# Issuing the transfers of SyncE's queue in written order, and placing loads, stores and the pieces of W1, W3 and W2 elsewhere in a step

## The chip, the cores and the metric

The kernel runs on one core of one Trainium2 chip. The metric is the device time of one execution in microseconds (us). The engines are TensorE (PE in the profile; its weight loads are PEld), VectorE (DVE), ScalarE (ACT), GpSimd (POOL) and SyncE (SP), which only issues transfers (DMAs).

## The reference

The model is one post-norm layer: gated slot attention, a layernorm over the residual sum, a gated FFN with a Hadamard transform, and a second layernorm. The input x has 2 batches of 2048 rows of 512 values, all fp32. The attention has 16 heads with 64 key features, 64 slots and 128 value features.

```python
q, k = heads(x @ Wq), heads(x @ Wk)                  # 64 wide
v = heads(x @ Wv); s = clip(heads(x @ Ws), -32, 32)  # 128 values, 64 slots
z = cumlogsumexp(s, time); g = exp(z_prev - z); p = exp(s - z)
hk = hk * g + k p^T;  ok = (q / 8) @ hk              # per time step
pv = softmax(ok)
hv = hv * g + p v^T;  o = pv @ hv                    # per time step
gate = x @ Wg
o = o * rsqrt(mean(o^2) + eps) * g_norm * silu(gate)
x = layernorm(x + o @ Wo)
h = fwht(silu(x @ W1^T) * (x @ W3^T))                # hidden 2048
out = layernorm(x + h @ W2^T)
```

## The kernel before

**Products of large matrices.** The projections, the output projection and the FFN's products are done in fp32 by a scheme with seven half-size products instead of eight. Each factor is cut in four blocks; VectorE forms sums of blocks of the weights and of x ahead of time (`first_sums`, `second_sums`, `right_sums`, `Weights.sums` at L408 and the lines beside it), TensorE makes the seven products in the order 1, 5, 6, 2, 7, 3, 4, and `Unit.into` takes each result from its PSUM bank: products 1, 5, 6 and 4 by ScalarE's copy, products 2, 7 and 3 by one VectorE addition each (L464) of the kept block. There are few PSUM banks for these, so a late addition holds a later product.

**Steps.** The 16 heads are done in NG = 4 groups of four, and the 2048 rows of time in NCB = 16 chunks of 128, for both batches at once. A group and a chunk make one `Step`, 64 in all, in order of groups. `run(new, now, before, old)` interleaves four steps. For `now` it makes the projections of q, k and the slot scores (`q(k)`, products at L504) and of v and the gate (`v(k)`, L530). For `new` it loads x and in the first group makes its block sums (`load_x`, `make_x`) and stores them to DRAM (`xd`, L488), from where later groups load them ready. For `before` it makes the gate, the softmax and the values. For `old` it makes the output projection (`o(k)`, L801), which adds to the partial rows: in the first group these are x itself, later the rows stored by the group before in `yd` (`load_rows` L748, `store_rows` L817).

**The burst.** Between product 1 and product 5 of v lies a run of small matmuls on 64x64 tiles: `scores` (L591), `scores2` (L681), `share_of_keys` (L607), `share_of_values` (L697), `slots` (L627), `values` (L710), `state_slots` (L636) and `state_values` (L719). These are 512 instructions of TensorE, matmuls and weight loads together, and take some 5 us. Keys, exponentials and weights need transposed copies for it. They are made by DMA transposes on 16-bit halves: GpSimd writes the halves (`parts`), SyncE issues the transpose (`rt` at L673, `kt` at L553, `et` at L564, `ot` at L769), ScalarE joins the halves (`kr` at L557). L607 is the first user of `kr`. `running_sum` also stores the last row of the running sum for the next step (`zc`, L579).

**Pieces.** Work that belongs to the FFN's weights is cut into pieces: generators that do some instructions and yield. `work()` runs them in order and `work_on(place)` takes the next one, at place 1 (in the q products), 2 (between q2 and q7), 3 (in the v products) and 4 (after v4). `up_weights` loads W1 and W3 in pieces of 1 MB (`both`), forms the block sums on VectorE (`outer`, `inner`) and stores them to DRAM (`w13s`, L853 to L856); it lies in the first group and the beginning of the second. `down_weights` multiplies W2 with a 128x128 Hadamard matrix (`product`, L909, 16 matmuls), does the other four butterfly levels on VectorE (L933, L935), forms the block sums (L941 to L944) and stores them (`w2s`); it lies in the second and third group. `block(j)` prepares the FFN's input from the normalised rows in the last group, with block sums on VectorE named `halves`. The FFN follows behind the last step (`up` at L238, `down` at L277).

**What sets the order.** The attention part stands in a block `tc.manual_schedule(engines={PE, DVE, Activation, Pool})`: on these four engines instructions are issued in the order in which the program writes them. SyncE is not in the set, so a scheduler of the build decides the order of the transfers on SyncE's queue by its own costs. An engine's queue is in order: an instruction that waits holds all behind it. The tail of the FFN has a second block of the same kind, which stays as it is.

The weights of the next group (`load_qks`, `load_vg`, `load_o`; `Weights` at L401, of which `low` is a shared buffer of one slot) are loaded when the group's last step comes (`last`; `o_last` for the output projection, two steps later), and the first step of a later group is called `changes`.

Of the kernel before, what the change touches and what calls it, by code (L numbers as in the profile page):

```python
# [24 lines left out]
NG = H // HG  # L25
# [14 lines left out]
def gated_slot_attention_ffn_kernel(  # L40
# [13 lines left out]
    nc = tc.nc  # L54
# [298 lines left out]
    with ExitStack() as att:  # L353
# [112 lines left out]
        class Step:  # L466
# [17 lines left out]
            def make_x(self):  # L484
                if self.g:
                    return
                right_sums(self.xb, self.b12)
                nc.sync.dma_start(out=xd[self.n], in_=self.xb)  # L488


            def q(self, k):
# [346 lines left out]
        def up_weights():  # L838

            todo = [(p, i) for p in range(NSET) for i in range(2)]  # L840

            def load(n):

                p, i = todo[n]
                nc.scalar.dma_start(out=both[:, n % 2].rearrange("p h q a b t -> p (h q a b t)"), in_=w13t[i, p])

            def inner(d, src, at, n):

                t = hp.tile([P, 4, 2, P], F32, name="inner", tag="h3", bufs=4)[:, :, 0:n]
                first_sums(nc.vector, t, *(src(r, c) for r in range(2) for c in range(2)))  # L850
                o = d[:, at : at + n].rearrange("p m k t -> p k m t")
                for c in range(2):
                    nc.sync.dma_start(out=o[:, c], in_=src(0, c))  # L853
                nc.sync.dma_start(out=o[:, 2], in_=src(1, 1))
                for k in range(4):
                    nc.sync.dma_start(out=o[:, 3 + k], in_=t[:, k])  # L856

            def sums(d, wt):

                outer = hp.tile([P, 4, 2, 2, P], F32, name="outer", tag="h2")  # L860
                a11, a12, a21, a22 = (wt[:, r, :, c] for r in range(2) for c in range(2))
                nc.vector.tensor_tensor(outer[:, 0], a21, a22, ALU.add)
                nc.vector.tensor_tensor(outer[:, 2], a11, a21, ALU.subtract)
                yield
                nc.vector.tensor_tensor(outer[:, 1], outer[:, 0], a11, ALU.subtract)
                nc.vector.tensor_tensor(outer[:, 3], a12, outer[:, 1], ALU.subtract)
                yield
                inner(d, lambda r, c: wt[:, 1, r, 1:2, c], 2, 1)
                yield
                inner(d, lambda r, c: outer[:, 0:2, r, c], 3, 2)  # L870
                yield
                inner(d, lambda r, c: outer[:, 2:4, r, c], 5, 2)
                yield
                inner(d, lambda r, c: wt[:, 0, r, :, c], 0, 2)

            both = hp.tile([P, 2, 2, 2, 2, 2, P], F32, name="both", tag="h1")
            rest = iter(())
            load(0)
            for n, (p, i) in enumerate(todo):
                for half in range(2):  # L880
                    for place in range(4):

                        if place == 3 and half:
                            for _ in rest:
                                pass
                            rest = sums(w13s[p][:, :, :, i], both[:, n % 2])
                        if place != 2:
                            next(rest, None)
                        if place == 3 and half and n + 1 < len(todo):
                            y["load"] = lambda n=n: load(n + 1)  # L890
                        yield
            for place in range(4):
                if place != 2:
                    next(rest, None)
                yield
            for place in range(4):
                if place != 2:
                    next(rest, None)
                yield

        def down_weights():
# [3 lines left out]
            for pair in ((0, 2), (1, 3)):  # L905
                wh = hp.tile([P, 2, NFB, P], F32, name="wh", tag="h1")

                def product(n, raw):
                    nc.tensor.matmul(bank(0), lhsT=hm, rhs=raw.rearrange("p (c t) -> p c t", t=P), start=True, stop=True)  # L909
                    nc.scalar.copy(wh[:, n // 4, n % 4 * 4 : n % 4 * 4 + 4], bank(0))  # L910
# [8 lines left out]
                for n in range(8):  # L919
                    yield  # L920
                    yield
                    yield
                    nraw = load(n + 1) if n < 7 else None
                    yield
                    product(n, raw)
                    raw = nraw
                for i in range(2):
# [127 lines left out]
        def run(new, now, before, old):  # L1055
# [13 lines left out]

            def work_on(place):  # L1070

                if changes or (last and place > 2) or (o_last and place == 3):
                    return
                y["place"] = place
                next(pieces[0], None)
# [25 lines left out]
            if new is not steps[1]:  # L1101
                do(new, "load_x")
            do(before, "tanh")
            main("q", 5)
            do(before, "squared_sums")
            do(before, "silu")
            y["second"] = new is not None and new.g > 0
            work_on(1)
            main("q", 6)
            if crossed:  # L1110
                old.o_joined()
# [6 lines left out]
            if crossed:  # L1118
                old.o_sums(True)
            main("q", 4)  # L1120
            if last:
                nw["qks"] = load_qks(g + 1)
            if now is steps[-1]:
                wt.append(load_w(0, 0))
                open_x("wqks", OUTER[:3], 3 * P)
# [25 lines left out]
                old.o(3)  # L1151
            do(old, "row_stats", 1)
            do(old, "o", 4)
            if old is not None and old.g < NG - 1:
                old.store_rows()
            do(now, "k_joined")
            y.pop("load", lambda: None)()
            if o_last:
                nw["o"] = load_o(old.g + 1)
            do(before, "load_rows")  # L1160

            do(now, "reciprocal", 0)
            do(now, "open_shares")
# [20 lines left out]
            do(before, "scaled")  # L1184

            do(old, "row_stats", 0)
            main("v", 5)
            for f in late:
                f(2)
# [12 lines left out]
            do(now, "softmax")  # L1202
            if old is not None and old.g == NG - 1:
                old.normalize()
                old.store_rows()
            if before is not steps[-1]:
                do(before, "o_split")
            do(now, "r_scaled")
            do(now, "r_split")
            if last:  # L1210
# [3 lines left out]
                for k in range(4):  # L1214
                    nw["o"].sums(k)
            main("v", 3)
            work_on(3)
            more()
            if before is steps[-1]:
                before.o_transposed()  # L1220
# [23 lines left out]
                    pieces[0] = chain(pieces[0], block(old.n // 4))  # L1244

        with tc.manual_schedule(
            engines={mybir.EngineType.PE, mybir.EngineType.DVE, mybir.EngineType.Activation, mybir.EngineType.Pool}
        ):
            steps[0].load_x()
            nw["qks"] = load_qks(0)  # L1250
            steps[1].load_x()
            nw["vg"] = load_vg(0)
            nw["o"] = load_o(0)
            steps[0].make_x()
            for k in range(4):
                nw["qks"].sums(k)
            N = len(steps)
            for i in range(N + 2):
                if i == N:
                    open_x("wvg", OUTER[3:], 4 * P)  # L1260
                    open_acc("ux", tag="h1")
                    ups = up(0, h)
                run(*(steps[j] if 0 <= j < N else None for j in (i + 1, i, i - 1, i - 2)))
            for _ in pieces[0]:
                pass
# [110 lines left out]
```

## Time and profile before

| | us |
|---|---|
| median of 3 runs | 3507.64 |
| lowest and highest run | 3504.44, 3511.28 |
| the profiled execution | 3514.42 |
| its span, first to last instruction | 3512.6 |
| mean granted TensorE clock in it | 0.988 |
| first matmul, end of the second step | 8.7, 85 |
| end of the first, second, third, last group | 642, 1212, 1791, 2383 |

How to read the profile: times count from the span's start. In a window's row the columns are start:end and length, then busy us and instructions of PE, PEld, DVE, ACT and POOL, the granted TensorE clock, the busy share of the core's 16 DMA engines, and GB/s. A row of waits names an engine, what it was about to write and the line, what it waited for, then us in total, times, longest. "issue" means that the engine waited for nothing that the profile shows. A row of the timeline has start, duration, engine, line, operation, out<-in, and in brackets the idle time ahead of it and what ended it. SPq is SyncE's queue: its durations are those of issuing, not of the transfer.

### The profile page before, as it was taken

To read this page: it belongs to the slowest core of one execution; us is meant where nothing else is said; L and a number is where in the kernel's file an instruction comes from. 1 tells how busy PE (TensorE), PEld (TensorE's weight loads), DVE (VectorE), ACT (ScalarE), POOL (GpSimd) and SP (SyncE) were. 2 spreads that over 40 slices of the span, in tenths; PEclk is the share of its full clock that TensorE was granted. 3 is DMA by queue.
4 is the path that set the end of the run, shared out by engine and by line. 5 is a ranking of instruction groups with operands and counts; after the bars stand their busy time and mean duration, and the time that the engine had idled before them with its cause. 6 is when DMAs were issued, how large, how long until landed. Compare 5 with 4: busy or idle time off the path is not lost.

```text
span 3512.6 us, 74754 instructions
## 1 busy us (share of the span) xinstructions
PE 3334.4 (95%) x30440; PEld 2631.8 (75%) x30440; DVE 2292.2 (65%) x3769; ACT 1306.4 (37%) x2939; POOL 1579.5 (45%) x1429
## 2 busy tenths in 40 slices
PE   7988988999999999999999999988999999999998
PEld 5766666777677766777677776766888888888887
DVE  4666656776556765556777677777666756756756
ACT  3444444454554554555455544542111111111110
POOL 2443444444444444444454444443634643643544
PEclk9999999999999999999999999999999999999999
DMA  5555555644443544434354565577455544445431
GB/s 170 145 154 145 144 143 151 175 120 119 93 108 92 149 111 116 104 97 106 95 150 112 123 161 158 163 204 254 172 180 206 176 160 177 154 154 182 163 135 68
DMA packets 542632, 508.40 MB, mean 145 GB/s; under 512 B 353488, under 2 KB 454224, under 8 KB 541264
## 3 DMA queue, kind: packets, MB, share of 16 engines
q1 hardware_dynamic: 541136, 495.23, 48.4%
q10 hardware_dynamic: 1152, 8.39, 0.8%
q8 instruction: 240, 3.93, 0.5%
q14 instruction: 104, 0.85, 0.1%
HBM read 297.47 MB, written 125.30 MB: 120 GB/s over the span
## 4 chain that ended last, share of the span: by engine, by line
PE 79%; DVE 9%; ACT 4%; issue 4%; DMA 2%; POOL 1%; SPq 0%; DVEq 0%; POOLq 0%; ACTq 0%
PE c L238 18%; PE c L530 18%; PE dc L277 11%; PE c L801 10%; PE c L504 9%; ACT r L654 2%; PE sp L719 2%; PE sp L710 2%; DVE t L464 2%; PE pv L697 2%; PE ps L573 1%; DMA kt<-parts 1%; PE ps L636 1%; PE sp L591 1%; DVE t L544 1%
## 5 line engine op out<-in xcount | busy, mean ns | idle before, releaser
L530 PE MATMUL c<-wvg,xb 128*128 128x512 f32 x1792 | 806.1, 601 | 7.8 <-DVE t L464 3.4
L530 PEld LDWEIGHTS c<-wvg,xb 128*128 128x128 f32 x1792 | 338.4, 192 | 396.8 <-issue 382.4
L504 PE MATMUL c<-xb,wqks 128*128 128x128 f32 x3584 | 556.5, 278 | 58.3 <-DVE t L464 45.4
L504 PEld LDWEIGHTS c<-xb,wqks 128*128 128x128 f32 x3584 | 477.2, 192 | 97.4 <-issue 55.1
L219 DVE TENSOR_TENSOR accux<-c,accux 128x512 f32<-128x512 f32 x496 | 341.1, 690 | 181.0 <-PE c L238 164.0
L277 PE MATMUL dc<-w2t,hid 128*128 128x256 f32 x1792 | 455.3, 379 | 2.1 <-DVE res L284 2.1
L238 PE MATMUL c<-wvg,xb 128*128 128x256 f32 x1792 | 431.9, 380 | 5.0 <-DVE accux L219 4.7
L238 PEld LDWEIGHTS c<-wvg,xb 128*128 128x128 f32 x1792 | 338.9, 190 | 55.6 <-DVE accux L219 8.5
L277 PEld LDWEIGHTS dc<-w2t,hid 128*128 128x128 f32 x1792 | 340.2, 190 | 49.5 <-DVE res L284 3.3
L504 PE MATMUL c<-wqks,xb 128*128 128x128 f32 x1792 | 348.1, 276 | 0.0
L238 PE MATMUL c<-wqks,xb 128*128 128x256 f32 x1344 | 327.8, 383 | 12.0 <-DVE accux L219 9.4
L464 DVE TENSOR_TENSOR t<-c,kept 128x384 f32<-128x384 f32 (+1 forms) x384 | 234.4, 619 | 147.7 <-PE c L530 87.4
L797 DVE TENSOR_TENSOR rows<-c,rows 128x256 f32<-128x256 f32 x448 | 189.4, 423 | 210.5 <-PE c L801 210.5
L238 PEld LDWEIGHTS c<-wqks,xb 128*128 128x128 f32 x1344 | 255.7, 191 | 51.5 <-DVE accux L219 11.8
L504 PEld LDWEIGHTS c<-wqks,xb 128*128 128x128 f32 x1792 | 273.3, 193 | 0.0
L284 DVE TENSOR_TENSOR res<-dc,res 128x256 f32<-128x256 f32 x448 | 189.1, 423 | 117.7 <-PE dc L277 107.3
L459 ACT COPY kept<-c 128x384 f32<-128x384 f32 (+1 forms) x384 | 202.9, 528 | 137.3 <-PE c L530 117.2
L584 DVE RECIPROCAL iz<-z 128x256 f32<-128x256 f32 x128 | 223.3, 1744 | 0.8 <-POOL xb L432 0.6
L544 DVE SCALAR_TENSOR_TENSOR t<-th,t 128x1024 f32<-128x1024 f32 x64 | 97.3, 1520 | 176.8 <-ACT th L540 176.8
L551 POOL COPY parts<-t 128x1024 uint16<-128x1024 uint16 x64 | 83.1, 1299 | 280.5 <-ACT t L461 271.4
L253 POOL TENSOR_TENSOR accw<-accw,accux 128x512 f32<-128x512 f32 x64 | 80.8, 1275 | 275.6 <-DVE accux L219 274.2
L737 POOL TENSOR_TENSOR ss<-ss,floor 128x8 f32<-128x8 f32 x64 | 13.0, 202 | 419.8 <-DVE ss L731 419.8
(194 smaller groups left out, 5622.9 us busy)
## 6 DMA issues: line engine op xcount, KB each, us to landing
xb<-w13s SPq DMA_DIRECT2D x112, 896.0 KB
xb<-xd SPq DMA_DIRECT2D x48, 896.0 KB
yd<-rows SPq DMA_DIRECT2D x128, 256.0 KB
w2t<-w2s SPq DMA_DIRECT2D x32, 896.0 KB
rows<-yd SPq DMA_DIRECT2D x100, 256.0 KB
xd<-xb SPq DMA_DIRECT2D x16, 896.0 KB
wvg<-fxd SPq DMA_DIRECT2D x16, 896.0 KB
w13s<-inner SPq DMA_DIRECT2D x96, 128.0 KB
```

Of the source, the lines that this page charges most:

```text
L219: nc.vector.tensor_tensor(into[:, b], s, (into if first is None else first)[:, b], ALU.add)
L238: nc.tensor.matmul(s[:, j * TQ : (j + 1) * TQ], lhsT=w[:, LEFT[k], j, :], rhs=right[:, RIGHT[k], :], start=(k in (1, 2, 5) and j == 0), st ...
L277: nc.tensor.matmul(s, lhsT=h["hid"][:, i, LEFT[m], k * P : (k + 1) * P], rhs=h["w2"][:, i, RIGHT[m], :], start=(m in (1, 2, 5) and i == 0) ...
L284: nc.vector.tensor_tensor(r, s, r, ALU.add)
L459: nc.scalar.copy(self.kept[k], s)
L464: nc.vector.tensor_tensor(t[:, to], s, self.kept[other], ALU.add)
L504: nc.tensor.matmul(out[:, i * P : (i + 1) * P], lhsT=a, rhs=b, start=(k in OPENS and c == 0 and i == 0), stop=(c == 1), skip_group_check=True,
L530: nc.tensor.matmul(out, lhsT=self.xb[:, RIGHT[k], c, :], rhs=w["vg"].t[:, LEFT[k], c, :], start=(k in OPENS and c == 0), stop=(c == 1), sk ...
L544: nc.vector.scalar_tensor_tensor(gate, self.th, 1.0, gate, ALU.add, ALU.mult)
L584: nc.vector.reciprocal(self.iz[:, h], self.z[:, h])
L797: nc.vector.tensor_tensor(y_, self.uo.sum(k), y_, ALU.add)
L801: nc.tensor.matmul(out, lhsT=self.ob[:, RIGHT[k], c, :], rhs=w["o"].t[:, LEFT[k], c, :], start=(k in OPENS and c == 0), stop=(c == 1), ski ...
```

## The change

SyncE joins the engines of the attention's `manual_schedule`, so that its transfers are issued in written order. With it, these are put at other places of the program:

- the store of x's block sums becomes a method of its own, `store_x`, which follows the burst (in the first step, the making of the sums);
- the load of `both` goes from ScalarE's queue to SyncE's;
- that load, the loads of the next group's weights `load_qks` and `load_o`, `store_rows` and `load_rows` stand behind the burst, ahead of product 5 of v; in the last group `store_rows` follows `o_split`;
- `work_on(1)` stands ahead of product 5 of q instead of behind the SiLU, and `work_on(3)` ahead of product 5 of v instead of behind product 3;
- `up_weights` leaves out place 2 instead of place 3 (its own count starts at 0, so `place != 1` there is the second place of a step);
- `down_weights` waits for place 1 with its Hadamard product;
- `work_on` also works in the first step of a group, and leaves out only place 4 where new weights come.

```diff
--- before.py
+++ after.py
@@ -485,7 +485,10 @@
                 if self.g:
                     return
                 right_sums(self.xb, self.b12)
-                nc.sync.dma_start(out=xd[self.n], in_=self.xb)
+
+            def store_x(self):
+                if not self.g:
+                    nc.sync.dma_start(out=xd[self.n], in_=self.xb)
 
 
             def q(self, k):
@@ -842,7 +845,7 @@
             def load(n):
 
                 p, i = todo[n]
-                nc.scalar.dma_start(out=both[:, n % 2].rearrange("p h q a b t -> p (h q a b t)"), in_=w13t[i, p])
+                nc.sync.dma_start(out=both[:, n % 2].rearrange("p h q a b t -> p (h q a b t)"), in_=w13t[i, p])
 
             def inner(d, src, at, n):
 
@@ -884,17 +887,17 @@
                             for _ in rest:
                                 pass
                             rest = sums(w13s[p][:, :, :, i], both[:, n % 2])
-                        if place != 2:
+                        if place != 1:
                             next(rest, None)
                         if place == 3 and half and n + 1 < len(todo):
                             y["load"] = lambda n=n: load(n + 1)
                         yield
             for place in range(4):
-                if place != 2:
+                if place != 1:
                     next(rest, None)
                 yield
             for place in range(4):
-                if place != 2:
+                if place != 1:
                     next(rest, None)
                 yield
 
@@ -922,6 +925,8 @@
                     yield
                     nraw = load(n + 1) if n < 7 else None
                     yield
+                    while y["place"] != 1:
+                        yield
                     product(n, raw)
                     raw = nraw
                 for i in range(2):
@@ -1069,7 +1074,7 @@
 
             def work_on(place):
 
-                if changes or (last and place > 2) or (o_last and place == 3):
+                if (last or o_last) and place == 4:
                     return
                 y["place"] = place
                 next(pieces[0], None)
@@ -1101,11 +1106,11 @@
             if new is not steps[1]:
                 do(new, "load_x")
             do(before, "tanh")
+            y["second"] = new is not None and new.g > 0
+            work_on(1)
             main("q", 5)
             do(before, "squared_sums")
             do(before, "silu")
-            y["second"] = new is not None and new.g > 0
-            work_on(1)
             main("q", 6)
             if crossed:
                 old.o_joined()
@@ -1118,8 +1123,6 @@
             if crossed:
                 old.o_sums(True)
             main("q", 4)
-            if last:
-                nw["qks"] = load_qks(g + 1)
             if now is steps[-1]:
                 wt.append(load_w(0, 0))
                 open_x("wqks", OUTER[:3], 3 * P)
@@ -1151,13 +1154,7 @@
                 old.o(3)
             do(old, "row_stats", 1)
             do(old, "o", 4)
-            if old is not None and old.g < NG - 1:
-                old.store_rows()
             do(now, "k_joined")
-            y.pop("load", lambda: None)()
-            if o_last:
-                nw["o"] = load_o(old.g + 1)
-            do(before, "load_rows")
 
             do(now, "reciprocal", 0)
             do(now, "open_shares")
@@ -1184,6 +1181,16 @@
             do(before, "scaled")
 
             do(old, "row_stats", 0)
+            if last:
+                nw["qks"] = load_qks(g + 1)
+            if o_last:
+                nw["o"] = load_o(old.g + 1)
+            if old is not None and old.g < NG - 1:
+                old.store_rows()
+            do(before, "load_rows")
+            y.pop("load", lambda: None)()
+            do(new, "store_x")
+            work_on(3)
             main("v", 5)
             for f in late:
                 f(2)
@@ -1202,9 +1209,10 @@
             do(now, "softmax")
             if old is not None and old.g == NG - 1:
                 old.normalize()
-                old.store_rows()
             if before is not steps[-1]:
                 do(before, "o_split")
+            if old is not None and old.g == NG - 1:
+                old.store_rows()
             do(now, "r_scaled")
             do(now, "r_split")
             if last:
@@ -1214,7 +1222,6 @@
                 for k in range(4):
                     nw["o"].sums(k)
             main("v", 3)
-            work_on(3)
             more()
             if before is steps[-1]:
                 before.o_transposed()
@@ -1244,7 +1251,7 @@
                     pieces[0] = chain(pieces[0], block(old.n // 4))
 
         with tc.manual_schedule(
-            engines={mybir.EngineType.PE, mybir.EngineType.DVE, mybir.EngineType.Activation, mybir.EngineType.Pool}
+            engines={mybir.EngineType.PE, mybir.EngineType.DVE, mybir.EngineType.Activation, mybir.EngineType.Pool, mybir.EngineType.SP}
         ):
             steps[0].load_x()
             nw["qks"] = load_qks(0)
@@ -1252,6 +1259,7 @@
             nw["vg"] = load_vg(0)
             nw["o"] = load_o(0)
             steps[0].make_x()
+            steps[0].store_x()
             for k in range(4):
                 nw["qks"].sums(k)
             N = len(steps)
```

## The prediction

> **What bounds the kernel.** I read the page's busy shares first, then the windows by stage, then who PE waited for in the first group, then single steps. TensorE carries the time:
>
> ```profile
> PE 3334.4 (95%) x30440; PEld 2631.8 (75%) x30440; DVE 2292.2 (65%) x3769; ACT 1306.4 (37%) x2939; POOL 1579.5 (45%) x1429
> 8.70:85.00 76.30, 60.01 (x584) 42.96 (x585) 42.12 (x50) 27.74 (x62) 19.24 (x18) 0.93 0.56 167
> 85.00:642.00 557.00, 500.42 (x5586) 375.43 (x5585) 354.11 (x603) 248.46 (x591) 236.07 (x207) 0.96 0.54 150
> 642.00:1212.00 570.00, 554.03 (x6353) 415.79 (x6352) 364.07 (x563) 289.58 (x684) 249.12 (x208) 1.00 0.46 115
> 1791.00:2383.00 592.00, 564.19 (x6435) 425.79 (x6434) 433.06 (x702) 296.40 (x695) 279.51 (x282) 0.99 0.58 153
> 2383.00:3513.00 1130.00, 1099.04 (x5135) 954.22 (x5133) 732.78 (x1297) 153.22 (x229) 530.72 (x476) 0.99 0.48 169
> ```
>
> After the page's line, these are windows from the first matmul over steps 0 and 1, steps 2 to 15, the second and the last head group, and the FFN; the figure after the five engines is the granted clock. The change edits only the attention part, so the FFN's 1130 us stay. What can be won is idle PE time and lost clock. Steps 2 to 15 hold most: 557.00 − 500.42 = 56.6 us idle, and (1 − 0.96) × 557 = 22 us lost to the clock. The second group idles 16 us, the last 28.
>
> The waits of PE in that stage:
>
> ```profile
> PE c L504 <- DVE t L464: 20.4, 13, 2.1
> PE sp L710 <- issue: 12.0, 3, 4.5
> PE ps L636 <- issue: 8.7, 3, 3.7
> PE sp L719 <- issue: 7.8, 3, 3.8
> PE ps L627 <- issue: 4.0, 2, 2.8
> PE c L530 <- issue: 2.4, 1, 2.4
> ```
>
> Two causes. First, 20.4 us before projection products (L504): the PSUM bank isn't free, since VectorE's add (L464) is late behind a piece of W1/W3. Second, 34.9 us of "issue" (12.0 + 8.7 + 7.8 + 4.0 + 2.4), nearly all in the burst of 512 small matmuls and weight loads (L591 to L719): nothing in the trace is late but PE's own instructions. Step 14, SyncE's queue and then PE:
>
> ```profile
> 580.90 1.23 SPq L553 DMA_TRANSPOSE kt<-parts  x1
> 584.95 0.39 SPq L748 DMA_DIRECT2D rows<-in_L_attn_hidden_states  x1
> 585.44 0.37 SPq L488 DMA_DIRECT2D xd<-xb  x1
> 585.91 1.61 SPq L817 DMA_DIRECT2D yd<-rows  x2
> 592.11 0.80 SPq L748 DMA_DIRECT2D rows<-yd  x2
> 592.37 1.65 PE L710 MATMUL sp<-t,a 64*64 64x128 f32 x25 [3.33 <-issue]
> ```
>
> rows, xd (896 KB) and yd are issued just ahead of the burst. The page has 240 instruction packets, 3.93 MB: 16 KB or some 256 of the 60,880 PE and weight-load instructions each, so the burst eats two packets in about 5 us. In this step the packet lands only after that backlog has drained, and PE restarts at 592.37. Steps whose backlog also has the 1 MB load of W1/W3 (the odd ones) stall longer, up to 4.5.
>
> **The change, part by part.** PE, VectorE, ScalarE and GpSimd keep their work; eight DMA issues move from ScalarE's queue to SyncE's.
>
> 1. Pieces of W1/W3 leave the place between q2 and q7 (place 2) for the v products (place 3), and place 1 goes ahead of the SiLU. The 20.4 us go if no other add is late. Bounds: all back at place 3, or all gone. An inner sum of 1.15 to 2.2 us now stands before the v2 add, which has some 0.8 us before v4 needs its bank: 0 to 0.9 per step, 0 to 12.6 over 14 steps; I take 2, since v products (1.98 us for four matmuls) leave more time than q's. **−20.4 + 2 = −18.4.**
>
> 2. SyncE in written order, step 0. The fourth load of Wo (low, L401) needs the buffer that VectorE's L408 reads. The scheduler put it behind kt; in the written order it stands before xd and kt:
>
> ```profile
> 23.19 2.69 SPq L553 DMA_TRANSPOSE kt<-parts  x1
> 28.68 0.27 PE L607 MATMUL pk<-e,kr 64*64 64x64 f32 x1 [2.22 <-ACT kr L557]
> 30.85 1.75 DVE L408 TENSOR_TENSOR wvg<-wvg,low 128x1024 f32<-128x1024 f32 x1
> 32.62 0.33 SPq L401 DMA_DIRECT2D low<-wo_blocks  x1
> ```
>
> The load can't issue before 32.60. With 0.33 for it and 0.37 for xd, kt goes at about 33.4, 10.2 after 23.19, and the burst waits directly for kt, transposed and copied (kr): +10.2, less up to 1.5 if the transpose takes 1.23 as in step 14 and not 2.69. Queued behind kt are et, zc, rows and the next x, all needed later. **+9.4** (8.7 to 10.2; 0 if that sum comes early). In step 1 kt stands behind a rows load that waits for VectorE; in the new order it doesn't. Its stall is 4.07 now: **−3** (−4.1 to 0).
>
> 3. Loads and rows "behind the burst". In the new order rows, both (the W1/W3 load), yd and xd come after kt, et, zc. But SyncE waits only for data, not for the burst: none of them reads what the burst makes. It reaches them at about the burst's start −1 to +1.5 us, where they stand now within −1.6 to +0.6. I queued the backlog again in the new order, by the trace's packets (7 KB take 0.28 us on each of 16 engines, 400 KB per us; 512 B take 0.03, some 250): the stalls sum to 34.8 instead of 34.9. **0**, bounds −34.9 (all gone) and +8.
>
>    The Trainium skill's page "DMA: Bandwidth & Descriptors", in the section "Queues, rings and completion order", says that each DMA engine serves its queues in turn, one packet each; by that rule an instruction packet never waits for a backlog on another queue, the order on SyncE is worth nothing, and bringing `both` over from ScalarE's queue takes away one competitor. The row of 3.33 us in step 14 speaks for a drain instead, so I keep the −34.9 as a bound.
>
> 4. kt's cover in steps 2 to 15. Between the transposes rt and kt SyncE now issues up to 14 stores of w13s and three x loads; at 0.43 to 0.5 us each, 17 take 8 us of the 9.7 us (571.2 to 580.90) between rt and kt in step 14. They fit, barely. **+1** (0 to 10).
>
> 5. Steps that change weights. Step 16 now has pieces, and wvg's three loads, low, x and 14 stores stand between rt and kt: 2.5 on VectorE and 1.5 on kr. Step 32 loses 2, steps 17 and 18 lose 1.5, since after one more piece in step 16 an inner sum again falls between q2 and q7. Sum 7.5, of which step 18's present 1.46 stall is part: **+6** (0 to 12). The Hadamard product (16 matmuls) moves from place 4 to place 1: same matmuls, **0** (±1).
>
> 6. W2's sums. Their stores hold VectorE in a few steps:
>
> ```profile
> 1334.10 1.22 PE L504 MATMUL c<-xb,wqks 128*128 128x128 f32 x4 [5.23 <-DVE t L464]
> ```
>
>    With the product tied to place 1, the sums spread over other places. At stake are this 5.23 and 3.25 in step 50: **−5** (−8.5 to 0).
>
> 7. Last group: rows and three fxd stores move to the burst, where the fetch may lose up to 1.2 in each of 7 steps, and "halves" now precede the v2 add; against that kt is freer in steps 54 and 58 (kr stalls 3.11 and 3.52). **+4** (−4 to +10).
>
> 8. Clock. Twelve windows of 3.41 us at half speed lie in steps 2 to 15, each after PE gaps that sum to 1.8 us or more. With item 1's gaps gone I expect two or three fewer at 1.7 us each: **−4** (−20 if item 3's stalls vanish, +5). The skill's "TensorE: Matmul & The Clock Gate" (Part 1, the clock gate) asks for one idle window of about 3.4 us; only three stalls here exceed that (3.7, 3.8, 4.5), so by it most windows have no cause and this term is 0.
>
> Sum: −18.4 + 9.4 − 3 + 0 + 1 + 6 + 0 − 5 + 4 − 4 = **−10**. Against the profiled execution's own 3514.42 that is 3504.4; the median of the runs, 3507.64, lies 6.8 lower, and there it is **3497.6**.
>
> **Rivals.**
>
> *A: the drain really moves.* If the large transfers land after the second instruction packet, item 3 gives about −27 of its −34.9 and item 8 another −12: −10 − 39 gives some 3459. For it: in step 9, with the same burst, PE has no issue stall at all. Against it: SyncE doesn't wait for the burst.
>
> *B: kt at the head of the line, slower.* One queue in written order means whatever waits ahead of kt holds the burst of every step. Price: a missed burst costs its delay directly, as step 1's 4.07 does now. If the 17 issues of item 4 take 0.6 us and not 0.47, they need 10.2 of the 9.7 us, and every step with 14 stores (seven of them) is late by 0.5 plus its conversion; yd, which waits for VectorE's o4 add and stands ahead of the next rows, both and xd, pushes the next ot too. The sum turns at +10: 1.4 us in each of the seven steps. At 3 to 4 us in each, +21 to +28 over my sum: 3518 to 3526, point 3522.
>
> *C: nothing to be measured.* Item 1's stall moves to the v products (its +12.6), all else as forecast: about 0, 3508. For it: VectorE's work is the same, and its share is 64% in those steps. Against it: v products are longer than q's.
>
> **How the numbers follow.** Forecast 0.40, A 0.20, B 0.28, C 0.12. 0.2% (7 us) is about what a measurement of this kernel can tell from no change. The forecast's own range is ±14 (3484 to 3512), the roots of the terms' bounds added. Faster by over 0.2% is below 3500.6: six tenths of the forecast and all of A, 0.24 + 0.20, some of C, 0.02: 0.46. Slower, above 3514.7: nearly all of B and little else, 0.31. Same: 0.23. The range leaves out a part of A and a part of B: 3458 to 3528.
>
> **What would show it.** Right: PE's L504 waits for L464 in steps 2 to 15 fall from 20.4 to under 4; "issue" there stays within 27 to 43; L607's wait for kr in step 0 grows from 2.2 to about 11; clock 0.96 to 0.97. Wrong towards A: "issue" under 15 and a clock of 0.99. Wrong towards B: L607's waits for kr over 1 us in many steps. Towards C: L530 waits for L464.

## The result: 1.8% slower

| | before | after |
|---|---|---|
| median, us | 3509.46 | 3573.34 |
| lowest to highest, us | 3504.44 to 3513.65 | 3569.42 to 3574.84 |
| profiled execution, its span, us | 3514.42, 3512.6 | 3572.38, 3570.6 |
| mean granted TensorE clock | 0.988 | 0.983 |

Four runs each; the ratio is 1.0181, with a 95% interval from 1.0163 to 1.0199. The forecast was 3497.6, with a range from 3458 to 3528: 10 us faster, where the kernel became 64 us slower. Further down, each ratio is against executions of the kernel before taken together with that run. One of run 11's four executions, at a granted clock of 0.653, took 4910.40 us and is left out of its median.

The page's busy line and the windows of the profile after, cut at the same places of the program (steps 0 and 1; 2 to 15; the second, third and last head group, the last up to the FFN; the FFN):

```profile
PE 3346.5 (94%) x30440; PEld 2635.8 (74%) x30440; DVE 2328.7 (65%) x3769; ACT 1307.8 (37%) x2939; POOL 1568.0 (44%) x1429
9.10:94.50 85.40, 61.35 (x584) 44.26 (x585) 41.60 (x50) 28.13 (x64) 19.20 (x18) 0.90 0.38 121
94.50:639.00 544.50, 492.17 (x5586) 365.64 (x5585) 387.62 (x602) 247.47 (x584) 236.00 (x207) 0.98 0.56 152
639.00:1224.80 585.80, 555.27 (x6353) 417.14 (x6352) 374.98 (x567) 290.25 (x687) 249.31 (x208) 1.00 0.44 113
1224.80:1813.20 588.40, 559.34 (x6354) 419.76 (x6353) 371.25 (x570) 289.88 (x684) 265.55 (x240) 0.99 0.44 115
1813.20:2437.80 624.60, 578.77 (x6437) 434.24 (x6435) 423.02 (x687) 297.50 (x695) 267.15 (x268) 0.96 0.51 142
2437.80:3570.00 1132.20, 1099.60 (x5133) 954.80 (x5132) 729.46 (x1295) 153.30 (x229) 527.81 (x475) 0.99 0.48 169
```

PE's work is the same number of instructions. Steps 2 to 15 are 12.2 us shorter than before (544.5 against 556.7 between the same two matmuls), and their clock is higher. All else in the attention is longer: steps 0 and 1 by 8.7, the second group by 16 (585.8 against 570), the third by 9 (588.4 against 579), and the last by 33 (624.6 against 592, clock 0.96 against 0.99).

Who PE waited for, first in steps 2 to 15, then in the second and third group, then in the last group:

```profile
PE c L533 <- DVE t L464: 28.1, 13, 2.6
PE pk L610 <- ACT kr L560: 6.0, 6, 1.7
PE sp L722 <- issue: 5.7, 3, 2.5
...
PE c L507 <- DVE t L464: 12.8, 8, 4.9
PE ps L639 <- issue: 11.0, 7, 1.9
PE sp L713 <- issue: 10.6, 6, 2.5
PE ps L630 <- issue: 7.5, 5, 2.0
PE sp L722 <- issue: 6.5, 6, 1.5
...
PE c L533 <- DVE t L464: 16.6, 7, 2.8
PE c L507 <- DVE t L464: 11.6, 4, 7.1
PE pk L610 <- ACT kr L560: 6.8, 3, 4.0
```

(Lines after L487 are three higher than before: L504 became L507, L530 L533, L607 L610.) The wait of the q products for VectorE's add, 20.4 us in steps 2 to 15, is gone there. A wait of the v products for it, 28.1, has come, and one of the q products for ScalarE's copy, 4.8. "issue" in those steps fell from 34.9 to 13.2, but in the next two groups (steps 16 to 47) it rose from 21.2 to 35.6. There it was, in the kernel before:

```profile
PE ps L627 <- issue: 8.3, 6, 2.0
PE sp L719 <- issue: 4.7, 4, 2.1
PE ps L636 <- issue: 4.2, 8, 0.9
PE sp L710 <- issue: 3.9, 5, 0.9
```

Two stretches of the profile after show what is new. In step 13, VectorE, then GpSimd, then PE:

```profile
556.27 0.29 DVE L829 TENSOR_TENSOR inner<-both 128x128 f32<-128x128 f32 x1
556.48 1.99 DVE L830 TENSOR_TENSOR inner<-both 128x128 f32<-128x128 f32 x1
558.39 0.28 DVE L831 TENSOR_TENSOR inner<-inner,both 128x128 f32<-128x128 f32 x1
558.70 1.86 DVE L832 TENSOR_TENSOR inner<-both,inner 128x128 f32<-128x128 f32 x1
560.49 1.28 DVE L464 TENSOR_TENSOR t<-c,kept 128x512 f32<-128x512 f32 x2
...
556.39 1.93 POOL L743 TENSOR_TENSOR t<-t,ss 128x1024 f32<-128x1024 f32 x1
558.38 2.04 POOL L770 COPY parts<-t 128x2048 uint16<-128x2048 uint16 x1
...
561.82 1.98 PE L533 MATMUL c<-wvg,xb 128*128 128x512 f32 x4 [1.98 <-DVE t L464]
```

Two of the four sums of a piece at place 3 take 1.9 us instead of 0.28, each beside one GpSimd instruction. v2's add (L464) stands behind the four on VectorE, and PE waits for the add. And in step 59, SyncE, VectorE, PE:

```profile
2227.19 1.34 SPq L820 DMA_DIRECT2D yd<-rows  x2
2230.06 1.25 SPq L676 DMA_TRANSPOSE rt<-parts  x1
2231.40 2.58 SPq L972 DMA_DIRECT2D yb<-yT  x4
2234.07 0.56 SPq L474 DMA_DIRECT2D xb<-xd  x1
2234.69 0.44 SPq L1013 DMA_DIRECT2D fxd<-yq  x1
...
2240.69 0.69 DVE L1019 TENSOR_TENSOR yq<-yq 128x512 f32<-128x512 f32 x1 [7.98 <-DMA fxd<-yq]
...
2241.91 1.22 PE L507 MATMUL c<-xb,wqks 128*128 128x128 f32 x4 [7.11 <-DVE t L464]
```

The store of yq stands behind yd, rt, four yb stores and a load. VectorE's next piece overwrites yq (the outer differences of `block`), so it waits 7.98 us for the store to land; q's add is behind it on VectorE, and PE waits 7.11.

### The profile page after: what moved, and what is told of

It is laid out like the page before. It is cut to its first block, busy times and chain, and to the rows that moved or that the text cites. A ratio compares the mean times of both kernels' runs of the same rounds, so it can differ in the third digit from the quotient of the medians.

```text
span 3570.6 us, 74633 instructions
## 1 busy us (share of the span) xinstructions
PE 3346.5 (94%) x30440; PEld 2635.8 (74%) x30440; DVE 2328.7 (65%) x3769; ACT 1307.8 (37%) x2939; POOL 1568.0 (44%) x1429
## 4 chain that ended last, share of the span: by engine, by line
PE 77%; DVE 9%; issue 5%; ACT 4%; DMA 3%; POOL 2%; SPq 1%; POOLq 0%; DVEq 0%; ACTq 0%
PE c L238 18%; PE c L533 14%; PE c L507 14%; PE dc L277 10%; PE c L804 9%; PE sp L722 2%; DMA kt<-parts 2%; PE sp L713 2%; PE pv L700 2%; DVE t L736 1%; DVE t L464 1%; PE ps L576 1%; ACT sq L732 1%; ACT r L657 1%; PE ps L639 1%
## 5 line engine op out<-in xcount | busy, mean ns | idle before, releaser
L533 PE MATMUL c<-wvg,xb 128*128 128x512 f32 x1792 | 819.3, 607 | 53.5 <-DVE t L464 51.3
L533 PEld LDWEIGHTS c<-wvg,xb 128*128 128x128 f32 x1792 | 337.6, 192 | 450.0 <-issue 370.4
L507 PE MATMUL c<-xb,wqks 128*128 128x128 f32 x3584 | 561.2, 280 | 42.8 <-DVE t L464 24.4
L507 PEld LDWEIGHTS c<-xb,wqks 128*128 128x128 f32 x3584 | 486.2, 195 | 86.0 <-issue 49.3
L507 PE MATMUL c<-wqks,xb 128*128 128x128 f32 x1792 | 350.7, 278 | 0.0
L464 DVE TENSOR_TENSOR t<-c,kept 128x384 f32<-128x384 f32 (+1 forms) x384 | 235.9, 620 | 169.7 <-PE c L507 109.3
L238 PE MATMUL c<-wqks,xb 128*128 128x256 f32 x1344 | 328.4, 383 | 13.6 <-DVE accux L219 10.2
L238 PEld LDWEIGHTS c<-wqks,xb 128*128 128x128 f32 x1344 | 256.0, 192 | 53.2 <-DVE accux L219 12.6
L507 PEld LDWEIGHTS c<-wqks,xb 128*128 128x128 f32 x1792 | 276.4, 195 | 0.0
L459 ACT COPY kept<-c 128x384 f32<-128x384 f32 (+1 forms) x384 | 203.5, 530 | 128.5 <-PE c L533 98.7
L663 POOL TENSOR_TENSOR r<-r,iz 128x512 f32<-128x512 f32 x64 | 84.6, 1322 | 266.4 <-ACT r L657 205.4
```

What stands on the lines that cost most here:

```text
L238: nc.tensor.matmul(s[:, j * TQ : (j + 1) * TQ], lhsT=w[:, LEFT[k], j, :], rhs=right[:, RIGHT[k], :], start=(k in (1, 2, 5) and j == 0), st ...
L459: nc.scalar.copy(self.kept[k], s)
L464: nc.vector.tensor_tensor(t[:, to], s, self.kept[other], ALU.add)
L507: nc.tensor.matmul(out[:, i * P : (i + 1) * P], lhsT=a, rhs=b, start=(k in OPENS and c == 0 and i == 0), stop=(c == 1), skip_group_check=True,
L533: nc.tensor.matmul(out, lhsT=self.xb[:, RIGHT[k], c, :], rhs=w["vg"].t[:, LEFT[k], c, :], start=(k in OPENS and c == 0), stop=(c == 1), sk ...
```

## The experiments

Theory P was, going in: the pieces ahead of v2's add are the loss. Theory Q: SyncE's single queue in written order is the loss. Each kernel is told as edits against the kernel before, the changed one, or an earlier run.

**1. Only the transfers changed.** The pieces are put back:

```diff
-            y["second"] = new is not None and new.g > 0
-            work_on(1)
             main("q", 5)
             do(before, "squared_sums")
             do(before, "silu")
+            y["second"] = new is not None and new.g > 0
+            work_on(1)
...
-            work_on(3)
             main("v", 5)
...
             main("v", 3)
+            work_on(3)
...
-                        if place != 1:
+                        if place != 2:
... (the same at two more places)
-                    while y["place"] != 1:
-                        yield
...
-                if (last or o_last) and place == 4:
+                if changes or (last and place > 2) or (o_last and place == 3):
```

> The changed kernel, but the pieces are taken where the kernel before took them (place 1 behind the SiLU, place 3 behind v3, place 3 left idle, the Hadamard product where it was); only SyncE's order and the places of loads and stores stay changed. Theory P (an inner sum or the halves ahead of v2's add, stretched from 0.28 to 2 us where they run beside GpSimd's product and copy, hold the v products): the 51 us that v products wait for VectorE's add fall under 8, the q products' 20 us in the first group come back, step 0 stays 13 us longer: 3508 to 3522. Theory Q (SyncE's one queue in written order is the loss): 3550 or more.

Measured: 3566.66, ratio 1.0163 (1.0134 to 1.0192). As P said, the v products wait 3.4 us for the add and q's wait returns (20.2 in steps 2 to 15), but the time is Q's.

**2. Only the pieces changed:** the kernel before with the same edits the other way round.

> The kernel before, with only the pieces at the places of the changed kernel; SyncE's order stays the scheduler's. Theory P: -20 for the q products in the first group, +28 for the v products there, +33 in the last group, some +8 around step 16: 3540 to 3565. Theory Q: 3495 to 3515.

Measured: 3524.64, ratio 1.0038 (1.0025 to 1.0052). Neither theory's number. Steps by stage, in us against the kernel before (from step start to step start in the profiles):

| steps | before | after | transfers alone | pieces alone |
|---|---|---|---|---|
| 0 and 1 | 76.7 | +8.7 | +16.0 | +0.5 |
| 2 to 15 | 556.7 | -12.2 | -26.1 | +4.3 |
| 16 to 53 | 1364.9 | +21.6 | +31.4 | -5.7 |
| 54 to 62 | 336.2 | +36.1 | +31.1 | +13.8 |
| sum | 2334.5 | +54.2 | +52.4 | +12.9 |

So both halves lose, 57 and 15 us of median. The order of the transfers wins 26 us where W1 and W3 are prepared, and loses everywhere else. These are single profiles: runs 6 and 8 below have the same program as run 1 in steps 2 to 15 and show -21.6 and -16.3 there, so this stage is known to some 10 us only. The pieces give back in steps 2 to 15 what they win (the v products' wait there is 20.7).

**3. Place 3 behind v3** in the changed kernel:

```diff
-            work_on(3)
             main("v", 5)
...
             main("v", 3)
+            work_on(3)
```

> The changed kernel with one edit: place 3 is taken behind v3 again, ahead of v4, so that v2's, v7's and v3's adds stand ahead of the piece; place 2 stays idle. Theory P: v products' waits for the add fall from 51 to under 10 and the last group comes back by 20 to 33: 3510 to 3530. If the pieces cost the same at any place of v, or the loss is in the transfers: 3560 or more.

Measured: 3564.56, ratio 1.0153 (1.0127 to 1.0179). The v products' wait fell from 51.3 to 3.4, but the time by 9 only. Steps 2 to 15 did gain 14 us (-26.0 against -12.2). There the wait moved:

```profile
PE pk L610 <- ACT kr L560: 27.8, 6, 5.5
```

A later piece issues its stores later, so they stand between rt and kt (run 11 has place 3 here too, but holds these stores back, and has no such wait). In the last group the q products wait 36.1 us for the add, and VectorE 42.2 for the yq stores.

**4. Step 0's load of Wo** in the changed kernel. With `True` the constructor loads three blocks only, and `load_low()` loads the fourth:

```diff
             for f in late:
                 f(3)
+            if now is steps[0]:
+                nw["o"].load_low()
...
-            nw["o"] = load_o(0)
+            nw["o"] = load_o(0, True)
```

> The changed kernel with one edit: in step 0 the fourth load of Wo (low) is issued behind v7, not ahead of kt. If that load alone holds kt: L610's wait for kr in step 0 falls from 13.2 to some 2, step 0 from 51.4 to 39, time 3557 to 3565. If something else holds kt next: over 3568.

Measured: 3569.79, ratio 1.0166 (1.0139 to 1.0192). kt now goes at 25.77, ahead of the load (35.20), the wait for kr in step 0 falls from 13.2 to 1.9, and step 0 from 51.4 to 39.9. That this load held kt is shown. The time is 3.6 us lower than the changed kernel's, not the 8 to 16 expected: of the 11.6 us, 3 are lost again in step 1 and 5.7 in steps 54 to 62. The waits for kr in the last group grew there from 6.8 to 11.8; why was not settled.

**5. GpSimd cleared from place 3** in the changed kernel; GpSimd's scaling of the gated values is left out, as the expectation says:

```diff
-                nc.gpsimd.tensor_tensor(self.gj, self.gj, ssb, ALU.mult)
...
-                nc.gpsimd.tensor_copy(parts, gated)
+                nc.scalar.copy(parts, gated)
```

> The changed kernel with GpSimd taken off the stretch in which place 3 now lies: its product of the gated values with 1/norm is left out (so the output is not the reference's), and its copy of their 16-bit halves is made by ScalarE. Pieces stay ahead of v5. Theory P1 (VectorE's sums with two SBUF operands stand still beside GpSimd's instructions): the 128x128 inner sum falls from 1.99 and 1.86 us to some 0.28, the halves from 1.1 to 0.42, and the 51 us that v products wait for the add fall under 12. Theory P2 (the sums are simply one piece too many ahead of v2's add, or slowed by the transfers beside them): the sums keep 1.9 us, or become short and the waits stay over 30.

The inner sums in steps 2 to 15, first of the changed kernel, then of this one (columns: busy us in all, mean ns of one, idle before):

```profile
L830 DVE TENSOR_TENSOR inner<-both 128x128 f32<-128x128 f32 x7 | 13.9, 1985 | 0.0
L832 DVE TENSOR_TENSOR inner<-both,inner 128x128 f32<-128x128 f32 x7 | 13.0, 1860 | 0.2
...
L829 DVE TENSOR_TENSOR inner<-both 128x128 f32<-128x128 f32 x7 | 2.0, 283 | 0.0
L831 DVE TENSOR_TENSOR inner<-both,inner 128x128 f32<-128x128 f32 x7 | 2.0, 292 | 0.2
```

1985 ns become 283 and 1860 become 292; in the last group the slowest of the four sums on the halves falls from 1065 to some 480. The v products wait 1.2 us for the add in the whole kernel, not 51.3. P1 holds: the stretch comes with GpSimd's two instructions (which of the two matters more was not tested); SyncE's transfers were issued in the same order. The time itself, 3642.7 us in a single execution, says nothing on this: the q products now wait 90.6 us for ScalarE's `kept` (L459).

**6. The yq stores on ScalarE**, on top of run 1:

```diff
-                nc.sync.dma_start(out=o[:, 0:2], in_=src[:, :, 0])
-                nc.sync.dma_start(out=o[:, 2], in_=src[:, 1, 1])
+                nc.scalar.dma_start(out=o[:, 0:2], in_=src[:, :, 0])
+                nc.scalar.dma_start(out=o[:, 2], in_=src[:, 1, 1])
```

> SyncE in written order with the pieces as before (the run of the pieces as before), and one more edit: the two stores of yq to fxd (L1013, L1014) are issued by ScalarE. Theory S1 (in written order these stores stand behind yd, rt, yb and x, and VectorE's outer differences, which overwrite yq, wait for them: 36.9 us in the last group): that wait falls under 5, q products' wait for the add in the last group from 33 to under 8, time lower by 20 to 32: 3535 to 3547. Theory S2 (the last group is held by kt or by the fetch): lower by under 8.

Measured: 3552.05, ratio 1.0114 (1.0094 to 1.0134), 14.6 below run 1. VectorE's wait for these stores, in the whole kernel, fell from 41.8 to 4.1 us, and steps 54 to 62 from +31.1 to +9.9. That shows S1 as the cause of most of that stage's loss. The gain is smaller than expected because a new wait came in the last group, 14.6 us for ScalarE:

```profile
PE c L507 <- ACT kept L459: 14.6, 5, 5.4
```

**7. Rows ahead of kt** in the later groups, in the changed kernel:

```diff
+            if before is not None and before.g:
+                before.load_rows()
             do(now, "k_split")
...
-            do(before, "load_rows")
+            if before is not None and not before.g:
+                before.load_rows()
```

> The changed kernel, but in the second to last group the loads of rows (512 KB) are issued ahead of kt instead of behind yd at the burst. Theory F (PE's instruction packets land behind what SyncE issued just ahead of the burst): issue in steps 16 to 53 falls from 35.6 to 22 to 28, steps 17 to 47 lower by 6 to 12. If the packets do not wait for the backlog: within 3 of 35.6.

The 35.6 us are those of steps 16 to 47, not to 53 as the expectation has it. There "issue" fell to 14.6, further than expected and below the 21.2 of the kernel before:

```profile
PE ps L630 <- issue: 6.5, 3, 3.3
PE sp L713 <- issue: 4.3, 6, 1.2
PE ps L639 <- issue: 2.8, 6, 0.7
```

Steps 16 to 53 went from +21.6 to +8.6 us (one profile of each). So PE's instruction packets did come behind what SyncE issued just ahead of the burst: moving the loads behind kt had put 512 KB of rows right behind the 512 KB of yd. The one execution took 3568.32 us, only 5 below the changed kernel, and the place ahead of kt goes with a new cost: PE's waits for kr rose from 32.0 to 46.9 us in the whole kernel, in the last group from 6.8 to 19.3.

**8. The three repairs together**, on top of run 1: those of runs 4, 6 and 7.

> SyncE in written order and the transfers at the changed kernel's places, pieces as before, with three repairs: step 0's low of Wo behind v7, the two yq stores on ScalarE, rows of the later groups ahead of kt. If the three are the costs of the order: the -26 us of steps 2 to 15 stay, step 0 is back, the last group within 5 of before: 3490 to 3510 against 3509. If each repair only uncovers another wait on the one queue: 3525 or more.

Measured: 3523.35, ratio 1.0042 (1.0027 to 1.0057): between the two numbers. Step 0 is back (0.0), but steps 2 to 15 show only 16.3 of the 26 us. PE waits 13.4 there for kr (8.3 in run 1 and 11.1 in run 6, with the same program in these steps); w13s stores still stand between rt and kt. Steps 54 to 62 are 14.7 longer, with waits of 12.4 for kr and 8.9 for ScalarE's `kept`.

**9. Stores held back.** Run 8's repairs of step 0 and of the rows (for the second and third group), the yq stores on SyncE again, and the edit below, made for all stores of w13s; `release()` issues what is held, behind the burst:

```diff
-                    nc.sync.dma_start(out=o[:, c], in_=src(0, c))
+                    held.append((o[:, c], src(0, c)))
...
             inner(0, b11)
             yield
+            inner(2, b22)
+            yield
             yield from outer(b11, b12, b11)
...
-            inner(2, b22)
+            inner(1, b21)
             yield
             yield from outer(b22, b22, b11)
             inner(4, b22)
             yield
-            inner(1, b21)
-            yield
             yield from outer(b21, b21, b22)
...
-            do(before, "load_rows")
+            if before is not None and before.g not in (1, 2):
+                before.load_rows()
+            release()
             y.pop("load", lambda: None)()
```

> SyncE in written order, pieces as before, step 0's low behind v7, rows of the second and third group ahead of kt; and in place of the yq stores on ScalarE: all w13s stores of a step are held and issued together behind the burst, so that none stands between rt and kt, and in the last group b22's inner sums go ahead of b11's differences, so that one piece lies between each yq store and VectorE's overwriting. If the queue's order ahead of kt and of yq is the rest of the loss: kr waits in steps 2 to 15 from 13 to under 4, the last group within 5 of before, 3475 to 3500. If the held stores only crowd ot, rt or the instruction packets: 3510 or more.

Measured: 3494.01, ratio 0.9958 (0.9944 to 0.9973): faster than the kernel before. kr no longer holds the burst in steps 2 to 15 (no such wait is left), which are 30.1 us shorter than before, and steps 54 to 62 are within 2.5. It changes several things at once. The stages keep the w13s stores apart from the rest, since w13s is written in the first group and the beginning of the second, and yq in the last. In the last group three edits lie together (the yq stores on SyncE again, the order of the sums, the rows behind the burst again), and what each is worth was not separated; VectorE waits 2.4 us there for the yq stores, where run 1 had 36.9. Its waits in steps 2 to 15 (lines shifted again by six):

```profile
PE c L513 <- DVE t L470: 19.8, 13, 2.0
PE ps L645 <- issue: 5.7, 3, 2.0
PE sp L719 <- issue: 5.6, 3, 2.3
PE sp L728 <- issue: 4.0, 3, 1.5
PE ps L636 <- issue: 2.9, 2, 1.8
```

**10. `both` back on ScalarE**, on top of run 1, one line:

```diff
-                nc.sync.dma_start(out=both[:, n % 2].rearrange("p h q a b t -> p (h q a b t)"), in_=w13t[i, p])
+                nc.scalar.dma_start(out=both[:, n % 2].rearrange("p h q a b t -> p (h q a b t)"), in_=w13t[i, p])
```

> The run of the pieces as before (SyncE in written order), with the 1 MB loads of W1/W3 back on ScalarE's queue, at the same place of the program. If the issuing queue matters to PE's instruction packets: issue in steps 2 to 15 moves from 10.8 by more than 5. If what counts is when the load is issued: within 4 of 10.8, and the time within 5 us of 3567.

Measured: 3570.87, ratio 1.0169 (1.0149 to 1.019), 4 us above run 1, and "issue" in steps 2 to 15 is 14.9 instead of 10.8. That is between the two expectations and no more than profiles differ: runs 6 and 8, with SyncE's queue and the same program in these steps, have 11.3 and 13.9. Which queue issues the 1 MB load makes no difference that was shown.

**11. The first term once more.** Run 9 with place 2 idle, and place 3 used behind v3 (one edit, at three places):

```diff
-                        if place != 2:
+                        if place != 1:
```

> The run with held stores, and W1/W3's pieces leave out place 2 instead of place 3; place 3 is behind v3, where no v add follows but v4's copy. If the forecast's first term holds once the piece is neither beside GpSimd's product and copy ahead of v2's add, nor its stores ahead of kt: the 19.8 us that q products wait for the add in steps 2 to 15 fall under 3, v products' stay under 3, kr under 3: 14 to 24 us below the run with held stores, 3470 to 3480. If the wait only moves again: 3488 or more.

Measured: 3477.83, ratio 0.9909 (0.9889 to 0.9928). The first line of run 9's waits became the third here:

```profile
PE sp L719 <- issue: 6.0, 3, 2.6
PE ps L645 <- issue: 5.4, 3, 2.1
PE c L513 <- DVE t L470: 4.6, 12, 0.5
```

19.8 us became 4.6, somewhat above the expected 3, there are no waits for v's add or for kr in these steps, and the time fell by 16. The term was real; the place that was chosen for the piece was not.

## Why the prediction was wrong, point by point

By stage, the forecast had +6.4 us in steps 0 and 1, -21.4 in steps 2 to 15, +1 in steps 16 to 53 and +4 in the last group. Measured were +8.7, -12.2, +21.6 and, in steps 54 to 62, +36.1. The steps that failed are item 7, where the moved yq stores were priced without VectorE's wait for them, 26.5 us, item 3, where the new backlog ahead of the burst in the later groups, "issue" +14.4, was put at nothing, and item 1, where the moved piece was priced as at its old place and cost the v products 28.1 us, not 2.

**Item 1 (-18.4).** The -20.4 came as forecast; the 2 for the v products did not: 28.1, beyond even the bound of 12.6. The price of an inner piece, "1.15 to 2.2 us", is that of its old places: at place 2 nothing of GpSimd's ran beside the sums of 128x128 (0.28 us each), at place 1 two short copies of GpSimd's did. At place 3 the piece takes 4.2 us (556.27 to 560.49), beside the product and copy that GpSimd makes there. The trace before had a warning in VectorE's groups of steps 2 to 15, where a sum of one shape has two prices:

```profile
L865 DVE TENSOR_TENSOR outer<-outer,both 128x512 f32<-128x512 f32 x7 | 8.4, 1193 | 0.0
L863 DVE TENSOR_TENSOR outer<-both 128x512 f32<-128x512 f32 x7 | 4.8, 685 | 0.0
```

All seven sums of L865 in these steps ran beside those copies (L778, L779); the eighth, at 752.04, did not and took 0.69 us. Run 5 shows the cause for the inner sums. The 4.8 us that the q products wait for ScalarE's copy had no place in the forecast; their cause stays open.

**Item 2 (+9.4 and -3).** The mechanism was right and the sizes nearly: step 0 +13.2, step 1 -4.5, together 8.7 where 6.4 stood. kt went at 35.62, not 33.4, because VectorE's L408 itself started at 33.48 instead of 30.85. That goes with the clock at the start, not with the change: it was granted in full from 18.53 us in this profile and from 11.90 in the one before; in runs 3, 6 and 7, where it was from 11.1 to 11.5 on, L408 starts at 30.6 to 30.7 and kt goes at 32.7 to 32.9. Behind the wait for kr the clock then stood at half for 17.07 us instead of 6.83, which the forecast did not price. Run 4 confirms the load.

**Item 3 (0).** Wrong twice, in opposite directions. In steps 2 to 15 "issue" fell by 21.7: SyncE reaches the transfers about when I said, in step 13 from 0.9 us ahead of the burst's start to 1.6 behind it, but that was not worth nothing. `both` and xd, 1.7 and 0.4 ahead of the burst in that step before, are issued 1.0 and 1.6 behind its start, and the first of the burst's two instruction packets gets ahead of them: in steps 11 to 14 it starts 3.6 to 5.1 us earlier in the step than before, and 1.2 to 3.1 us earlier against the burst's own start. Where PE stalls in these steps, in both profiles, it restarts 1.2 to 1.5 us after that packet's end. In steps 16 to 47 "issue" rose by 14.4, because yd and rows now stand together ahead of the burst (run 7). My model of the backlog covered the first group only; the other groups had 26.3 us, and the rows' new place was not priced there. In the first group this is what rival A forecast, and its sign, "issue" under 15, was met.

**Item 4 (+1).** 6.0, within its bounds of 0 to 10. Rival B named the mechanism and the place of head-of-line waiting; here it is small, and in run 3, with the stores issued later, it is 27.8.

**Items 5 and 6 (+6 and -5).** Step 16 lost 8.2, step 32 3.6, steps 17 and 18 together 2.5: 14.3, somewhat above the upper bound of 12. Of W2's steps, 33 to 35 moved by -0.6 and 48 to 53 by -3.7: -4.3, as forecast.

**Item 7 (+4).** The largest miss: +36.1, where the bound was +10. I moved fxd's stores and asked only what they do to the instruction packets. Who waits for these stores to land was not asked: VectorE, which overwrites yq one piece later. Before, that wait did not exist in the last group; after, it is 26.5 us in four waits, and 36.9 with the transfers alone (run 1), first and second line here:

```profile
DVE yq L1019 <- DMA fxd<-yq: 26.5, 4, 8.0
DVE yq L1017 <- DMA fxd<-yq: 36.9, 8, 6.9
```

The other part is item 1's stretch again, on the halves ahead of v2's add (16.6 us of v waits).

**Item 8 (-4).** The time lost to half clock (half the length of its windows) fell in steps 2 to 15 from 20.5 to 10.2 us, more than forecast, and rose in the last group from 5.1 to 22.2: in all a loss, where a gain was forecast. PE's idle time in the last group grew by 18 us (624.6 - 578.8 against 592 - 564.2), and its busy time, at the lower clock, by 14.6.

The rival that came closest was B, with the right sentence (whatever waits on one queue in written order holds what is behind it) and the wrong victim: not kt in the first group, but VectorE in the last. Rival C's sentence, that the wait moves to the v products, came true as well; its 12.6 us were 28.1.

## What to carry to other kernels

When a queue goes from a scheduler's order to the written one, list for every transfer on it who waits for its landing, overwriters too, and not only who waits for its data; here the costliest was a store whose source is overwritten one piece later. Hold stores that nobody waits for until the critical transfers are out, and give a store that has an overwriter one more piece of distance (runs 8 to 9, both together: 3523 to 3494). A piece of work that is moved has to be priced at its new place, with what the neighbour engines do there: the same sum cost 0.28 us at one place and 1.99 at the other.

## What the hardware showed that I had not expected

- VectorE's sums of two operands in SBUF stand still beside GpSimd's instructions: 1985 ns beside them, 283 without. An add of the same engine with one operand in PSUM (L464, 128x512) kept 0.69 us where it ran beside GpSimd's instructions (26 of 41 adds in steps 2 to 15 of the kernel before) and 0.68 where it did not. The Trainium skill's page "SBUF — State Buffer", in "Who interferes with whom", says just this: an instruction of VectorE with two SBUF inputs contends with one of GpSimd that reads SBUF, and the one that comes second blocks. I hadn't looked there for an edit that only moves VectorE's work.
- PE's instruction packets waited for a backlog of other transfers: moving 512 KB per step out of their way took "issue" from 35.6 to 14.6 us (run 7). The rule that the prediction weighed, of the Trainium skill's page "DMA: Bandwidth & Descriptors" ("Queues, rings and completion order"), one packet of each queue in turn, would by the prediction's reading have made no difference there; the measurement decides.
- A gap of under 3 us was followed by half clock: in step 60 of the changed kernel PE waited 2.81 us for the add, from 2306.7 on, and the granted clock stood at 0.5 from 2308.88 for 6.83 us.
